# First projection of layer 1's tokens as pieces beside layer 0's last 64 scan steps, patch permutation kept in DRAM

## The chip, the core and the metric

The kernel runs on one core of a Trainium2 chip. Its engines are TensorE (PE; weight loads are listed apart as PEld), VectorE (DVE), ScalarE (ACT), GpSimd (POOL) and SyncE (SP), which issues nearly all DMAs here. Each engine works through its own instructions in order and waits on semaphores for the others. The metric is the time of one execution on the device in microseconds, as the median of the runs.

## The reference

Input x is 4 images of 128 channels and 64 x 64 pixels, all in float32. Two layers follow each other, cut here to what bears on the change.

```
# layer 0, on a group-normalised x
order = argsort of the patches' scores                   # 256 patches of 4 x 4 pixels
x1n   = layer norm of (x in that order + pe)             # (4, 4096, 128)
xm, z = split(x1n @ in_proj_w.T)                         # 256 channels each
xc    = silu(causal conv of 4 taps over xm)
dt, B, C from xc
h_t   = exp(dt_t * A) * h_{t-1} + dt_t * B_t * xc_t      # 256 channels x 16 states
y     = (sum over states of h * C + D * xc) * silu(z)
x     = x + (y @ out_proj_w.T, patches put back in place)
# layer 1, on the tokens t of x
xs, z = split(layer_norm(t) @ W_in)                      # 256 channels each
delta = xs @ W_delta ; Bv = xs @ W_B ; Cv = xs @ W_C
state_t = exp(delta_t A) * state_{t-1} + delta_t Bv_t xs_t    # 256 channels x 256 states
t = t + ((sum over channels' states with Cv) * silu(z)) @ W_out
t = t + sum over 16 filters of causal convolutions of layer_norm(t), with matrices
```

## The kernel before

The program has three stages, one after the other.

**`layer0_front`** (L24) treats the four images in turn: statistics, convolutions, scores, and from these the permutation of the 256 patches as a matrix of zeros and ones. Its transpose goes into `perm_t` (L278), a tile of all four images that stays in SBUF in the pool `ordered` until layer 0 is done. The normalised tokens in their order go to DRAM as `xnt` (L293), one write of 2 MB for each image. The order of this stage's instructions is set by a scheduler.

**`layer0_scan`** (L336) has its order written out by hand. It loads its weights (L362 to L377: `win`, `taps`, `an`, `ow` and others; L356 is the load in the helper), then runs 512 steps: 32 units of 512 tokens (4 images by 8), each in 2 halves by 8 pairs of states. A step j issues the broadcast loads of B and C for step j + 5 (`fetch`, L526), the input products for step j + 3 on GpSimd (`spread`, L540), the factors for step j + 1 on ScalarE (`lift`, L554, four instructions), and the scan of step j on VectorE (`scan`: the scan L562, the product with C L566, a small copy L567). TensorE adds the products up in PSUM (`add_up`, L578, L584), and after eight steps VectorE multiplies with the gate (`gated`, L594). The two PSUM tiles of factors alternate, so that `lift` of a step waits for the scan two steps back.

Beside each step, `beside` (L618) advances pieces of other work. Such work is a generator that says what its next piece needs: "free" (nothing), "mm" (the one PSUM tile `mm`, for a group of matmuls) or "post" (the evacuation of that tile, one step later). `fronts` are projections of the coming units (`project`, L392), which begin 9 steps ahead; `rear` is the output of finished units (`output`, L462) and the return of a finished image to its place (`put_back`, L479, with `perm_t`). One holder has the `mm` tile at a time, fronts before rear. After the last step, what is left of this runs alone (L661), and the last image's rows `om` go to DRAM as `omd` (L664, two writes of 1 MB); its return to place is made by layer 1.

**`layer1`** (L772) has an order by hand too. Its own pools lie where those of layer 0's scan lay, so that a tile's first writer waits for those who last used that place. Its weights (`layer1_weights`, L758) are loaded much earlier, into the pool `const`. Before its steps it runs the projection of the first 512 tokens without anything beside it (L1290 to L1292): `project` (L862) loads the tokens from `x2` (L867), transposes them (L871), normalises (L828), transposes back (L881), and makes gate, u, c and delta by matmuls (L889, L899, L906, L915, L921), each with its evacuation; gate and delta go to DRAM (L894, L927). Then come 8192 steps, one for each of 32 parts and 256 channels d. The rows of delta are fetched as broadcasts over 128 partitions, two to a load, eight steps ahead (L1196). GpSimd multiplies them with u (L1212), ScalarE makes the factors (L1232), VectorE scans (L1235), TensorE contracts with c (L1252). The output of the last part, layer 0's return to place, and the projection of the next part run as pieces beside these steps (L1300), and so do the spectral convolutions (L1169, L1111).

SP issues the DMAs of all this in the order of the program. A load whose place or source is not ready holds up every DMA behind it.

Of the kernel before, what the change touches and what calls it, by code (L numbers as in the profile page):

```python
# [15 lines left out]
NB = 4  # L16
L = 4096
# [6 lines left out]
def layer0_front(ctx: ExitStack, tc, ident, half, w, x, xnt, perm_t, pqd, mud):  # L24
# [161 lines left out]
    def ordered(b, xg, x1, mvx, r1, m1):  # L186
# [87 lines left out]
        for h in range(2):  # L274
            tp = ps1.tile([128, 2, 128], F32, tag="one", name="tp1")
            for k in range(2):
                nc.tensor.transpose(tp[:, k, :], perm[:, k, bass.ts(h, 128)], ident)
            nc.vector.tensor_copy(perm_t[:, b, h, :], tp.rearrange("p k j -> p (k j)"))  # L278
# [57 lines left out]
def layer0_scan(ctx: ExitStack, tc, ident, w, x, xnt, perm_t, x2, omd):  # L336
# [25 lines left out]
    win = load("win", [128, 512], w["in_proj_w"])  # L362
    taps = load("taps", [128, 4, 256], w["conv1d_w"].partition_broadcast(128))
# [23 lines left out]
    def middle():  # L387
        return ps_.tile([128, 512], F32, tag="mm", name="mm")

# [72 lines left out]
    def output(b, unit, yg, om):  # L462

        yr = yg.rearrange("p k (r o) -> p k o r", o=16)
# [14 lines left out]
    def put_back(b, om):  # L479

        for h in range(2):
# [107 lines left out]
    def gated(j):  # L589
# [5 lines left out]
        if i == PJ // SUB - 1:  # L595
            b, unit = units[n]
            if unit == 0:
                oms[b] = big.tile([128, 2, 16, 128], F32, tag="om", name="om")
            behind.append(output(b, unit, ygs.pop(n), oms[b]))
            if unit == L // PJ - 1:  # L600
                if b < NB - 1:
                    behind.append(put_back(b, oms[b]))
# [12 lines left out]
    fronts, rear, holder = [], None, None  # L615
    ahead = [1]

    def beside(j):  # L618
# [5 lines left out]
        if ahead[0] < len(units) and j >= per * (ahead[0] - 1) - 9:  # L624
            ready[ahead[0]] = tiles()
            fronts.append(Work(project(*units[ahead[0]], ready[ahead[0]])))
            ahead[0] += 1
        while fronts and fronts[0].kind is None:
# [3 lines left out]
        for work in (*fronts, rear):  # L632
            if work and work.kind == "free":
                work.next()
        for work in (*fronts, rear):
# [25 lines left out]
    while holder or rear and rear.kind or behind:  # L661
# [109 lines left out]
@with_exitstack  # L771
def layer1(ctx: ExitStack, tc, ident, half, weights, phi, pqd, mud, x, omd, permd, x2, x3, out):  # L772

# [4 lines left out]
    ctx.enter_context(tc.manual_schedule())  # L789
    wp = ctx.enter_context(tc.tile_pool(name="s_w", bufs=1))  # L790
    big = ctx.enter_context(tc.tile_pool(name="s_big", bufs=2))
    sm = ctx.enter_context(tc.tile_pool(name="s_sm", bufs=2))
    wk = ctx.enter_context(tc.tile_pool(name="s_wk", bufs=2))
    sp = ctx.enter_context(tc.tile_pool(name="s_sp", bufs=3))
    dr = ctx.enter_context(tc.tile_pool(name="s_dr", bufs=2, space=DRAM))
    pa = ctx.enter_context(tc.tile_pool(name="s_pa", bufs=1, space=PSUM))
    pm = ctx.enter_context(tc.tile_pool(name="s_pm", bufs=1, space=PSUM))
    pc = ctx.enter_context(tc.tile_pool(name="s_pc", bufs=2, space=PSUM))
    pf = ctx.enter_context(tc.tile_pool(name="s_pf", bufs=1, space=PSUM))

    win, wbd, wc, wo, at = weights
    eps = wp.tile([128, 1], F32, name="eps")
    nc.vector.memset(eps, 1e-5)
    flip = wp.tile([128, 128], F32, name="flip")
    nc.vector.memset(flip, 0.0)
    nc.gpsimd.affine_select(
        out=flip, in_=flip, compare_op=ALU.not_equal, fill=1.0, base=-127, pattern=[[1, 128]],
        channel_multiplier=1,
    )
    halos = [wp.tile([128, 2], F32, name=f"halo{i}") for i in range(2)]  # L810
    lasts = [wp.tile([128, 2, 256], F32, name=f"last{i}") for i in range(2)]
    factors = [pa.tile([128, 2, TS], F32, name=f"da{i}") for i in range(2)]
    for da in factors:
# [649 lines left out]
```

## Time and profile before

| | us |
|---|---|
| median of 3 runs | 21432.37 (21429.57 to 21440.76) |
| the profiled execution's own time | 21431.38 |
| its span, from the first instruction to the last | 21429.6 |
| VectorE busy | 20566.6 (96%) |
| GpSimd busy | 20134.2 (94%) |
| TensorE busy | 17672.7 (82%) |
| ScalarE busy | 16044.5 (75%) |
| first matmul of layer 0's scan stage (L405) | at 555.9 |
| layer 0's last scan (L562) | at 2723.5 |
| layer 1's first scan (L1235) | at 2801.4 |

Rows of the profile that are shown below read as follows. In the chain of waits: start, length, and what the end of the program hung on at that time, an instruction, a transfer, or "issue", where nothing that the profile shows was waited for. In a timeline: start, length, engine, source line, operation, output and inputs with their sizes. In a window: its stretch and length, then busy time and instructions of PE, PEld, DVE, ACT and POOL, the granted clock of TensorE as a share of full speed, the busy share of the DMA engines, and GB/s. In the list of transfers: output and source, number, size, and the median time from issue to landing. In a group: busy time, mean of one in ns, and the idle time of the engine just before them with what ended it. The source lines are those of the kernel before.

### The profile page before, as it was taken

How to read it: one execution, taken by the hardware profiler on the slowest of the kernel's cores; microseconds unless marked ns; L12 is line 12 of the kernel's file. 1: busy time of each engine (PE TensorE's matmuls, PEld its weight loads, DVE VectorE, ACT ScalarE, POOL GpSimd, SP SyncE). 2: the span in 40 equal slices, each digit the busy share in tenths (PEclk: the TensorE clock that was granted, in tenths of full speed). 3: DMA queues.
4: the chain of work that ended last, by engine and by line, in shares of the span. 5: the costliest groups of instructions: out<-in, count | busy, mean ns of one | idle time of the engine just before them, and what ended most of it. 6: DMA issues, size and time to landing. Idle time of an engine off the chain costs nothing.

```text
span 21429.6 us, 294489 instructions
## 1 busy us (share of the span) xinstructions
PE 17672.7 (82%) x99308; PEld 7756.7 (36%) x99308; DVE 20566.6 (96%) x11871; ACT 16044.5 (75%) x29620; POOL 20134.2 (94%) x5685
## 2 busy tenths in 40 slices
PE   7788854565858888886868999599999999999997
PEld 4344421222323333342323344243434434334434
DVE  7788889999999999999999999999999999999996
ACT  3777767777777777777777777787887787788875
POOL 2677789999999999999999999999999999999996
PEclk8999966776979999998979999799999999999999
DMA  1455544555756777766657777577777777777776
GB/s 69 126 139 141 140 151 153 175 179 165 218 171 221 221 224 220 221 212 191 209 181 220 230 237 236 171 236 232 237 232 229 232 234 232 233 233 230 231 231 186
DMA packets 2498780, 4302.24 MB, mean 201 GB/s; under 512 B 803272, under 2 KB 1321712, under 8 KB 2494192
## 3 DMA queue, kind: packets, MB, share of 16 engines
q1 hardware_dynamic: 2497264, 4283.40, 65.4%
q8 instruction: 784, 12.85, 0.2%
q14 instruction: 732, 6.00, 0.1%
HBM read 3658.98 MB, written 623.38 MB: 200 GB/s over the span
## 4 chain that ended last, share of the span: by engine, by line
DVE 57%; PE 14%; POOL 9%; ACT 9%; issue 8%; DMA 3%; SPq 0%; DVEq 0%; POOLq 0%; ACTq 0%
DVE s L1235 50%; POOL v L1212 8%; PE conv L1169 6%; ACT da L1232 5%; DVE states L562 3%; PE yp L1252 3%; DVE p L566 2%; PE fin L1111 1%; ACT f L554 1%; PE y L578 1%; DMA strip<-in_phi 1%; DMA dlb<-delta 1%; PE mm L471 1%; PE conv L104 0%; DVE v L1224 0%
## 5 line engine op out<-in xcount | busy, mean ns | idle before, releaser
L1212 POOL TENSOR_TENSOR v<-u,dlb 128x2044 f32<-128x2044 f32 (+1 forms) x4096 | 18244.4, 4517 | 91.7 <-DMA dlb<-delta 66.0
L1235 DVE TENSOR_TENSOR_SCAN s<-da,v 128x1024 f32<-128x1024 f32 x8192 | 18006.6, 2264 | 188.3 <-ACT da L1232 130.3
L1232 ACT ACTIVATE da<-dlb,at 128x511 f32<-128x511 f32 x16384 | 11302.9, 690 | 1990.3 <-DVE s L1235 1488.8
L1169 PE MATMUL conv<-strip,tok 128*128 128x512 f32 (+3 forms) x20480 | 8653.3, 550 | 59.0 <-DMA strip<-in_phi 58.5
L1252 PE MATMUL yp<-s,c 128*32 128x256 f32 x65536 | 4957.0, 432 | 2616.2 <-DVE s L1235 1136.7
L1169 PEld LDWEIGHTS conv<-strip,tok 128*128 128x128 f32 x20480 | 3667.2, 192 | 4156.2 <-issue 3715.8
L1252 PEld LDWEIGHTS yp<-s,c 128*32 128x32 f32 x65536 | 1964.4, 120 | 6395.3 <-issue 2085.0
L1216 ACT COPY v<-vf 128x4 f32<-128x4 f32 x4096 | 814.2, 199 | 2112.6 <-DVE s L1235 2093.6
L1111 PE MATMUL fin<-conved,pq 128*128 128x512 f32 (+1 forms) x3968 | 1793.6, 545 | 11.1 <-ACT sum L1132 5.9
L540 POOL TENSOR_TENSOR v<-dx,bcb 128x1024 f32<-128x1024 f32 x512 | 1207.2, 2358 | 436.9 <-DVE states L562 430.5
L562 DVE TENSOR_TENSOR_SCAN states<-f,v 128x1024 f32<-128x1024 f32 x512 | 1175.8, 2297 | 172.6 <-ACT f L554 123.7
L554 ACT ACTIVATE f<-dt,an 128x255 f32<-128x255 f32 x2048 | 973.5, 476 | 418.0 <-DVE states L562 367.2
L1258 ACT COPY ye<-yp 128x512 f32<-128x512 f32 x2048 | 1186.1, 579 | 23.3 <-PE yp L1252 22.6
L1181 ACT COPY conved<-conv 128x512 f32<-128x512 f32 (+1 forms) x1728 | 986.9, 571 | 236.6 <-PE conv L1169 234.0
L578 PE MATMUL y<-p,ident 128*128 128x512 f32 x2048 | 1006.7, 620 | 148.2 <-DVE p L566 143.2
L1111 PEld LDWEIGHTS fin<-conved,pq 128*128 128x128 f32 x3968 | 664.2, 192 | 384.6 <-issue 284.2
L566 DVE TENSOR_TENSOR p<-states,bcb 128x1024 f32<-128x1024 f32 x512 | 626.9, 1224 | 41.1 <-DVE states L562 3.1
L578 PEld LDWEIGHTS y<-p,ident 128*128 128x128 f32 x2048 | 369.4, 195 | 680.9 <-issue 356.3
L471 PE MATMUL mm<-ow,yg 128*32 128x128 f32 x2048 | 283.1, 298 | 106.9 <-ACT om L475 105.4
L471 PEld LDWEIGHTS mm<-ow,yg 128*32 128x32 f32 x2048 | 236.6, 139 | 213.6 <-ACT om L475 128.5
L405 PE MATMUL mm<-xin,taps 128*128 128x512 f32 x512 | 236.6, 605 | 28.3 <-DVE f L384 14.4
L447 POOL TENSOR_TENSOR e<-e,e 128x1024 f32<-128x1024 f32 x32 | 75.1, 2346 | 191.0 <-ACT e L445 191.0
(242 smaller groups left out, 5948.1 us busy)
## 6 DMA issues: line engine op xcount, KB each, us to landing
dlb<-delta SPq DMA_DIRECT2D x4096, 512.0 KB, 4.2
strip<-in_phi SPq DMA_DIRECT2D x1536, 448.0 KB, 4.8
yd<-ye SPq DMA_DIRECT2D x2048, 256.0 KB, 4.1
strip<-in_phi SPq DMA_DIRECT2D x1088, 256.0 KB, 4.4
bcb<-bcd SPq DMA_DIRECT2D x1024, 256.0 KB, 4.1
pq<-pqd SPq DMA_DIRECT2D x1472, 64.0 KB, 3.8
yt<-yd SPq DMA_DIRECT2D x4096, 4.0 KB, 3.4
pq<-pqd SPq DMA_DIRECT2D x256, 128.0 KB, 3.9
```

The lines of the kernel that those rows point to most:

```text
L540: nc.gpsimd.tensor_tensor(v, ready[n][2][:, :, bass.ts(i, SUB)].unsqueeze(1).broadcast_to((128, 2, 2, SUB)), bc[:, 0].unsqueeze(2).broadca ...
L554: nc.scalar.activation(factors[j % 2][:, a, k, 1:], ready[n][1][:, k, SUB * i + 1 : SUB * i + SUB], AF.Exp, scale=an[:, k, 2 * g + a : 2 * ...
L562: nc.vector.tensor_tensor_scan(states.rearrange(flat), factors[j % 2].rearrange(flat), v.rearrange(flat), 0.0, ALU.mult, ALU.add)
L566: nc.vector.tensor_tensor(p, states, bc[:, 1].unsqueeze(2).broadcast_to((128, 2, 2, SUB)), ALU.mult)
L578: nc.tensor.matmul(t.rearrange("p k t -> p (k t)"), ident, p[:, a].rearrange("p k t -> p (k t)"), start=g == 0 and a == 0, stop=False, ski ...
L1111: nc.tensor.matmul(fin[:, bass.ds(c0, w)], pq[:, n, :], u[:, bass.ds(c0, w)], start=begin and n == 0, stop=end and not partly, skip_group_ ...
L1169: nc.tensor.matmul(ps[:, skip:], tok[:, 1 - r if side else r, j, :], strip[:, bass.ds(c0 - lo, TS - skip)], start=which == 0 and j == js[0 ...
L1212: nc.gpsimd.tensor_tensor(v[:, 0:n, :, 1:], ready[0][:, :, 1:].unsqueeze(1).broadcast_to((128, n, 2, TS - 1)), dl[:, 0:n, 1:].unsqueeze(2) ...
L1232: nc.scalar.activation(da[:, h, 1:], dl[:, d % VD, 1:], AF.Exp, scale=at[:, h, d : d + 1])
L1235: nc.vector.tensor_tensor_scan(s[:, d % GD].rearrange("p h t -> p (h t)"), da.rearrange("p h t -> p (h t)"), v[:, d % VD].rearrange("p h t ...
L1252: nc.tensor.matmul(yp[i // 2][bass.ts(q, 32), i % 2], c[:, h, t], s[:, :, h, t], start=h == 0, stop=h == 1)
L1258: nc.scalar.copy(ye, yp[j].rearrange("p i d t -> p i t d"))
```

## The change

Layer 1's `project` and what it needs (`small`, `wide`, `normalise`, `tiles`) move out of `layer1` into a function `projection`, which is called before layer 0's scan and has pools of its own that outlive both layers. One set of the tiles u, c, vf is made there, a second one in layer 1's pool at the second part. Which PSUM tile `middle` gives is taken from a list: layer 0's `mm` first, layer 1's own later. The generator of the first projection is handed to `layer0_scan`, which starts it at step 448 as `extra`, after fronts and rear in the order of choice; `layer1` no longer runs it.

`perm_t` no longer stays in SBUF from the front. Each half of each image's transposed permutation is written to DRAM as it is made, and layer 0's scan loads all of it (1 MB) with its weights. Layer 1's weights move from the pool `const` to a pool opened after the front. The tile `om` has one buffer in place of two and is allocated in `output`.

```diff
@@ layer0_front
-            nc.vector.tensor_copy(perm_t[:, b, h, :], tp.rearrange("p k j -> p (k j)"))
+            pt = sm.tile([128, 256], F32, tag="pt", name="pt")
+            nc.vector.tensor_copy(pt, tp.rearrange("p k j -> p (k j)"))
+            nc.sync.dma_start(permd[:, b, h, :], pt)
@@ layer0_scan
     win = load("win", [128, 512], w["in_proj_w"])
+    perm_t = load("perm_t", [128, NB, 2, 256], permd)
     taps = load("taps", [128, 4, 256], w["conv1d_w"].partition_broadcast(128))
...
+    psum.append(middle)
...
-    def output(b, unit, yg, om):
+    def output(b, unit, yg):
+        if unit == 0:
+            oms[b] = big.tile([128, 2, 16, 128], F32, tag="om", name="om", bufs=1)
+        om = oms[b]
...
+        if j == steps - 64:
+            extra.append(Work(following))
...
-        for work in (*fronts, rear):
+        for work in (*fronts, rear, *extra):
             if work and work.kind == "free":
                 work.next()
-        for work in (*fronts, rear):
+        for work in (*fronts, rear, *extra):
             if work and work.kind == "mm" and holder is None:
                 work.next()
                 holder = work
...
-    while holder or rear and rear.kind or behind:
+    while holder or extra[0].kind or rear and rear.kind or behind:
         beside(steps)
@@ projection, new, around the old project
+def projection(ctx, tc, ident, half, weights, x2, psum, second):
+    first = ctx.enter_context(tc.tile_pool(name="p_1", bufs=1))
+    sm = ctx.enter_context(tc.tile_pool(name="p_sm", bufs=2))
+    dr = ctx.enter_context(tc.tile_pool(name="p_dr", bufs=2, space=DRAM))
...
     def middle():
-        return pm.tile([128, TS], F32, tag="mm", name="mm")
+        return psum[0]()
...
+    def set_of(pool):
+        return [pool.tile(shape, F32, name=name) for name, shape in (
+            ("u", [128, 2, TS]), ("c", [128, 2, TS]), ("vf", [128, 2, 256]),
+        )]
+    af = first.tile([128, 2, 256], F32, name="af")
+    sets = [set_of(first)]
+    def tiles(n):
+        if n and len(sets) < 2:
+            sets.append(set_of(second[0]))
+        u, c, vf = sets[n % 2]
...
@@ layer1
-    ready = {0: tiles()}
-    for _ in project(*parts[0], ready[0]):
-        pass
+    ready = {0: first}
@@ conv_attn_hybrid
-    with tc.tile_pool(name="ordered", bufs=1) as pool:
...
-        layer0_front(tc, ident, half, w, x, xnt, perm_t, pqd, mud)
-        weights = layer1_weights(nc, const, *(w[k] for k in ("W_in", "W_delta", "W_B", "W_C", "W_out", "A")))
...
-        nc.sync.dma_start(permd, perm_t[:, NB - 1])
-        layer0_scan(tc, ident, w, x, xnt, perm_t, x2, omd)
-    layer1(tc, ident, half, weights, w["phi"], pqd, mud, x, omd, permd, x2, x3, out)
+    layer0_front(tc, ident, half, w, x, xnt, permd, pqd, mud)
+    pool = ctx.enter_context(tc.tile_pool(name="weights", bufs=1))
+    weights = layer1_weights(nc, pool, *(w[k] for k in ("W_in", "W_delta", "W_B", "W_C", "W_out", "A")))
+    psum, second = [], []
+    work = projection(ctx, tc, ident, half, weights, x2, psum, second)
+    first = work[-2](0)
+    layer0_scan(tc, ident, w, x, xnt, permd, x2, omd, psum, work[-1](0, 0, first))
+    layer1(tc, ident, weights, work, psum, second, w["phi"], pqd, mud, x, omd, permd, first, x2, x3, out)
```

## The prediction

> **What bounds the kernel now.** I read the page's chain first, to see which stage owns the time:
>
> ```profile
> DVE s L1235 50%; POOL v L1212 8%; PE conv L1169 6%; ACT da L1232 5%; DVE states L562 3%; PE yp L1252 3%; DVE p L566 2%; PE fin L1111 1%; ACT f L554 1%; PE y L578 1%; DMA strip<-in_phi 1%; DMA dlb<-delta 1%; PE mm L471 1%; PE conv L104 0%; DVE v L1224 0%
> L1235 DVE TENSOR_TENSOR_SCAN s<-da,v 128x1024 f32<-128x1024 f32 x8192 | 18006.6, 2264 | 188.3 <-ACT da L1232 130.3
> ```
>
> Layer 1's 8192 scans (L1235) fill VectorE from 2801 us to the end: 18006.6 us busy, 188.3 us idle ahead of them. The change adds nothing to that loop. So I read the two seams: the end of layer 0's scan, and the start of that scan (where the diff adds loads). The first, as the chain of waits, gives start and length:
>
> ```profile
> 2725.90 1.24 DVE p L566
> ...
> 2740.76 0.58 ACT om L475
> 2741.36 3.85 DMA omd<-om
> ...
> 2791.56 0.32 SPq L927
> ...
> 2791.97 4.72 DMA dlb<-delta
> ...
> 2796.85 4.51 POOL v L1212
> 2801.38 2.29 DVE s L1235
> ```
>
> Layer 0's last product ends at 2727.1 and layer 1's first scan starts at 2801.4. In between lie the last output rows (to 2741.3), the write of om, the projection of layer 1's first 512 tokens, one broadcast load and one product. Between steps, layer 0's last 17 show a period of 3.81 us, with this busy time by engine (PE, PE loads, DVE, ACT, POOL):
>
> ```profile
> 2662.00:2727.00 65.00, 42.57 (x140) 19.73 (x140) 61.83 (x52) 31.21 (x66) 34.87 (x31) 1.00 0.40 114
> ```
>
> VectorE has 95%, the others about half: there is room for a projection, but not on VectorE.
>
> **Part 1, what goes: the projection at the seam.** In the changed program all pieces stand before step 497 of 512: u at steps 488 and 489, the last af at 495. Their tiles now lie outside both layers' own pools, so nothing of the projection is left at the seam. What stays is a wait: SP's first dlb load has to see both om writes landed, because dlb lies where om lay, as xq's load did before. om's second write is issued at 2741.36 and SP goes on at 2745.39 (4.03 us). Then the load 2791.97 to 2796.72 (4.75), 0.13 to start, and the product 4.51, to the scan at 0.02: 13.44 in all. First scan at 2754.80 instead of 2801.38: **-46.6 us**. Behind that waiting load on SP stand only the other dlb loads, which are wanted later. The memset and select of flip now precede the first product on VectorE and GpSimd, but end long before dlb lands. Bounds: -44.3 if the om write takes the 6.3 us of its slower half, -47.6 if the load lands in 3.7 us, the median around this seam.
>
> **Part 2, what moves: the same instructions beside the scan.** VectorE, which has no room, gets four bn_stats (0.87), four aggregates (0.36), two u (2 x 0.69) and four af (2 x 0.49): 3.6 us, counted in full. GpSimd gets 1.2 us against about 1.1 us idle in every step, with v three steps ahead: hidden. TensorE gets under 29 us in 43 steps while about a third of it is idle. SP gets five DMAs between bcb loads that run five steps ahead: hidden. ScalarE gets 13.5 us: ten copies of 0.58, two statistics 0.5, the four normalisations 1.65, silu 1.06, two table loads 2.57, vf 1.24, exp 0.63.
>
> ScalarE is where a page speaks against the change. A lift (2.0 us) may begin when the scan two steps back ends, and is needed 5.3 us later. The row of layer 0's own silu:
>
> ```profile
> 2594.86 1.28 ACT L418 ACT_TABLE_LOAD   x1
> 2596.15 1.91 ACT L418 ACTIVATE xz<-xz 128x2048 f32<-128x2048 f32 x1
> 2598.08 1.28 ACT L554 ACT_TABLE_LOAD   x1
> 2599.37 2.01 ACT L554 ACTIVATE f<-dt,an 128x255 f32<-128x255 f32 x4
> ```
>
> That is 4.5 us, and the step took 3.86 us against 3.81: no stall. The Trainium skill, "ScalarE: Activation LUTs", section "What ACT_TABLE_LOAD costs", gives about 1.28 us plus a drain of 1.38, 2.66 for every switch, and so advises to do all of one set before switching; this change puts a silu into a stream of exps. By the page its silu would cost 1.06 + 5.3 = 6.4 us and overrun ScalarE's slack of 3.3 us plus the 1.8 us that each step frees, by about 1.3 us. By the row no such drain appears (load 1.28, next instruction 0.01 later): 1.06 + 2.57 = 3.6 us, hidden. I take the row. A nearer measure of everything together: steps 480 to 496, with a unit's projection, took 64.3 us, and the next 16, without, about 61.7; that projection has some 13 us of ScalarE and 9.4 of GpSimd, and costs 2.6, nearly all of it at its Ln pair. The new pieces have no Ln; I take 0.9 us for them. Sum **+4.5 us**; bounds 3.6 (VectorE alone) and 17 (all of ScalarE's 13.5 exposed as well).
>
> **Part 3, what is added at the other seam: the start of layer 0's scan.** DMA queue of the stretch 500 to 620, median us to landing, and SP's wait:
>
> ```profile
> xnt<-xn SPq DMA_DIRECT2D x1, 2049.5 KB, 8.6
> xin<-xnt SPq DMA_DIRECT2D x2, 257.5 KB, 2.8
> taps<-in_conv1d_w SPq DMA_DIRECT2D x1, 512.0 KB, 9.0
> cb<-in_conv1d_b SPq DMA_DIRECT2D x1, 1.0 KB, 8.3
> SPq L397 <- DMA taps<-in_conv1d_w: 0.4, 1, 0.4
> ```
>
> One KB took 8.3 us because it stood behind 2 MB: the loads drain about in order. Here all engines wait: xnt is issued at 542.73 and landed by 551.3, taps at 552.65, xin is issued at 552.66 and TensorE begins at 555.91. The change puts three things in this path. Layer 1's five weight loads (1.125 MB) leave the first 25 us, where nothing waited for them, and stand behind xnt. perm_t (1 MB, new) stands ahead of taps. And layer 0's win now lies over the old xn tile, so its load, and every one behind it on SP, waits for xnt's landing; before, they were issued under it. So win, perm_t and taps (1.75 MB) start at 551.3, behind what is left of the weights. At 430 GB/s (the rate of the loads at the start) they drain by 556.6, at 270 (this stretch) by 560; with 1.7 us from last byte to landing, taps is there at 558.3 to 561.7. xin waits for taps (0.4 to issue, 2.8 to land): TensorE begins at 561.6 to 565.3. **+5.7 to +9.4, taken +7.5 us.** The ten issues (nine took 6.5 us before, and perm_t's) end at about 558 and are not the later limit. It cannot be much under +4: the wait for xnt is in the program.
>
> The eight small permd writes of the front (128 KB each) stand ahead of writes that wait longer for ScalarE: nothing. One om buffer instead of two: output and put_back were already one queue, nothing. perm_t resident or loaded is the same operand to put_back.
>
> **Sum**: -46.6 + 4.5 + 7.5 = -34.6 us. Against the profiled execution: span 21429.6 to 21395.0, its time 21431.4 (1.8 around the span) to 21396.8. The median of the three runs is 21432.4, 1.0 above; I forecast that minus 34.6: **21398 us**, or -0.16%. About 0.2% (43 us) is what a measurement of this kernel can tell from no change: the forecast lies inside it.
>
> **Rivals.**
> - *The pieces cost what their ScalarE time is.* If their copies fall where ScalarE is already late (the Ln pair delayed the scan by about 2 us in each unit), up to 17 us go in the 64 steps: -46.6 + 17 + 7.5 = -22, **21410**. For: VectorE waited for f 6.6 us in the last 65 steps. Against: those waits lie at six scans alone. 0.15.
> - *Both losses are hidden*: the start overlaps (SP's issues were stretched by a full queue, and taps comes in time), the pieces cost 3.6: -43, **21389**. Against: the ordered wait on xnt. 0.10.
> - *The long loop changes its pace, and the kernel is slower.* u, c, vf and the small tiles sit at other addresses, and the loop starts without the 70 us pause (granted clock 1.00 before it, 0.62 in 2800 to 2900). It decides from 34.6 us / 8192 = 4.2 ns a scan (0.19% of 2264); at 7 ns it gives +57 - 35 = +22, **21455**. Against: VectorE is 98.6 to 100% busy there at a clock of 0.6, so the clock has no say, and the loop's order of instructions is the same in both programs. 0.05.
> - *The moved part is not moved*: pieces left over at the end would run at the seam. The program's order excludes it; within the first rival.
>
> **Numbers.** Forecast 0.70, with its own 21390 to 21404. Range 21386 to 21413, which takes in the bounds of the parts and the first two rivals. Faster than 21389.5 (0.2%): 0.10, the second rival. Slower than 21475: 0.02, a part of the third, whose rest stays within. Within 0.2%: 0.88.
>
> **What would show it.** Right: from layer 0's last output copy to the first L1235 scan some 13.5 us (60.0 before); the first L405 matmul 6 to 9 us later than 555.9, SP's load of win waiting for xnt; the 64 steps 4 to 6 us longer, with bn_stats, u and af between the scans; the scans' mean still 2264 ns. Wrong: a first dlb load that waits for more than om; f late at more than the six scans; another mean at L1235.

## The result, and the profile after

| | before | changed |
|---|---|---|
| median, us | 21434.19 (21429.57 to 21441.05, 9 runs) | 21379.17 (21368.94 to 21383.9, 9 runs) |
| ratio | | 0.9972, 95% interval 0.9964 to 0.9981 |
| profiled execution, its time (span) | 21431.38 (21429.6) | 21379.17 (21377.5) |
| front's last copy (ScalarE) to layer 0's first taps matmul | 13.2 | 19.1 |
| layer 0's last 64 scans, first start to last start | 251.8 | 253.0 |
| layer 0's last scan to layer 1's first scan | 77.9 | 30.6 |
| layer 1's first scan to its last scan | 18448.2 | 18437.8 |
| last scan's end to the end | 177.8 | 171.4 |

The changed kernel is 55.0 us faster, a little over a quarter of a per cent. The forecast was 21398 us with a range that began at 21386 and a chance of 0.88 for "within 0.2%": the time fell under the range, and the gain is larger than 0.2%. The rows from the fourth on are differences of starts and ends in the two traces.

On the page of the changed kernel, the chain by line and the two largest groups (busy time, mean of one in ns, then idle time ahead and its cause):

```profile
DVE s L1261 50%; POOL v L1238 8%; PE conv L1195 7%; ACT da L1258 5%; PE yp L1278 3%; PE fin L1137 1%; DMA dlb<-delta 1%; DMA strip<-in_phi 1%; DMA yd<-ye 0%; DVE v L1250 0%; ACT ye L1284 0%; PE mm L1052 0%; ACT t L820 0%; PE mm L884 0%; DVE st L805 0%
...
L1238 POOL TENSOR_TENSOR v<-u,dlb 128x2044 f32<-128x2044 f32 (+1 forms) x4096 | 18223.6, 4518 | 66.2 <-DMA dlb<-delta 42.9
L1261 DVE TENSOR_TENSOR_SCAN s<-da,v 128x1024 f32<-128x1024 f32 x8192 | 18008.3, 2286 | 187.8 <-ACT da L1258 132.0
```

The picture is the old one, and the second line holds what the forecast did not weigh. It stood on the page before as well:

```profile
L1212 POOL TENSOR_TENSOR v<-u,dlb 128x2044 f32<-128x2044 f32 (+1 forms) x4096 | 18244.4, 4517 | 91.7 <-DMA dlb<-delta 66.0
```

GpSimd's 4096 products fill 18223.6 us with 66.2 us idle ahead of them, against 187.8 us ahead of the scans; before, it was 91.7 against 188.3. The chain does not tell who leads: it gives half of the time to the scans and 8% to the products. Both engines look full; here the one with less idle time sets the pace, as the experiments show.

The chain of waits at the end of layer 0 in the changed kernel (start, length, what):

```profile
2737.80 1.24 DVE p L575
...
2752.65 0.59 ACT om L483
2753.24 0.02 issue
2753.25 3.86 DMA omd<-om
...
2757.32 3.96 DMA dlb<-delta
...
2761.53 4.50 POOL v L1238
...
2766.06 0.04 DVE s L1261
```

The projection is gone from it. From the last copy of om to the first scan it takes 12.8 us: the store, one broadcast load, one product. The forecast had 13.4.

ScalarE beside the last 64 steps, in the timeline of the changed kernel (start, length, engine, line, operation, how many), at the moved silu:

```profile
2582.91 1.28 ACT L871 ACT_TABLE_LOAD   x1
2584.20 1.06 ACT L871 ACTIVATE t<-t 128x1024 f32<-128x1024 f32 x1
2585.28 1.28 ACT L563 ACT_TABLE_LOAD   x1
2586.57 3.93 ACT L563 ACTIVATE f<-dt,an 128x255 f32<-128x255 f32 x8
```

From the first table load to the first factor of the scan 3.66 us pass: 1.06 of silu and two loads of 1.28. No further pause stands at either switch. The row was the right choice against the 2.66 us a switch of the Trainium skill ("ScalarE: Activation LUTs", "What ACT_TABLE_LOAD costs").

At the start of layer 0's scan (stretch 500 to 620), the transfers of the changed kernel with KB and median us to landing:

```profile
xnt<-xn SPq DMA_DIRECT2D x1, 2049.5 KB, 8.3
perm_t<-permd SPq DMA_DIRECT2D x1, 1024.0 KB, 5.7
xin<-xnt SPq DMA_DIRECT2D x2, 257.5 KB, 2.9
taps<-in_conv1d_w SPq DMA_DIRECT2D x1, 512.0 KB, 6.6
```

and the waits of SP's queue there (line, what for, us in total, how often, longest):

```profile
SPq L358 <- DMA xnt<-xn: 2.9, 1, 2.9
SPq L358 <- DMA perm_t<-permd: 1.6, 1, 1.6
SPq L402 <- DMA taps<-in_conv1d_w: 1.0, 1, 1.0
```

By SP's own timeline it is win that stands 2.9 us for the landing of xnt, ow 1.6 us for that of perm_t, and xin 1.0 us for that of taps. The wait for xnt was forecast, and taps in front of xin. What the forecast did not see is a pattern: ow is the eighth load behind perm_t, and xin the eighth behind taps. Before, `an`, the eighth behind xnt, stood 2.2 us for xnt, and xin, again the eighth behind taps, 0.4 us. In after_start (below) ow is the eighth behind taps and waits for it (0.6 us), while xin, right behind taps, is issued at 554.36 without a wait. So win waits for its place, as forecast, and the other waits go by the place in SP's row.

Up to layer 1's first scan the changed kernel is 35.3 us ahead (2801.38 to 2766.06). 3.6 us of the other sign lie in the front, to which the change adds the writes of permd. They are spread and no cost of it: over the profiles of this study the front's last copy ends at 542.7 to 547.7 without the change and at 542.8 to 549.3 with it, with a median of 546.1 in both. The other 17 us lie inside layer 1, where the order of instructions is the same on every engine: 10.4 in the loop, 6.4 in the tail (after the last scan). These were the open question.

### The profile page after: what moved, and what is told of

Read it like the earlier page. It is cut to its first block, busy times and chain, and to the rows that moved or that the text cites. A ratio compares the mean times of both kernels' runs of the same rounds, so it can differ in the third digit from the quotient of the medians.

```text
span 21377.5 us, 294496 instructions
## 1 busy us (share of the span) xinstructions
PE 17653.8 (83%) x99308; PEld 7751.4 (36%) x99308; DVE 20559.4 (96%) x11871; ACT 16041.0 (75%) x29620; POOL 20113.6 (94%) x5685
## 4 chain that ended last, share of the span: by engine, by line
DVE 51%; PE 12%; POOL 8%; issue 7%; ACT 6%; DMA 2%; SPq 0%; DVEq 0%; POOLq 0%; ACTq 0%
DVE s L1261 50%; POOL v L1238 8%; PE conv L1195 7%; ACT da L1258 5%; PE yp L1278 3%; PE fin L1137 1%; DMA dlb<-delta 1%; DMA strip<-in_phi 1%; DMA yd<-ye 0%; DVE v L1250 0%; ACT ye L1284 0%; PE mm L1052 0%; ACT t L820 0%; PE mm L884 0%; DVE st L805 0%
## 5 line engine op out<-in xcount | busy, mean ns | idle before, releaser
L1238 POOL TENSOR_TENSOR v<-u,dlb 128x2044 f32<-128x2044 f32 (+1 forms) x4096 | 18223.6, 4518 | 66.2 <-DMA dlb<-delta 42.9
L1261 DVE TENSOR_TENSOR_SCAN s<-da,v 128x1024 f32<-128x1024 f32 x8192 | 18008.3, 2286 | 187.8 <-ACT da L1258 132.0
L1137 PE MATMUL fin<-conved,pq 128*128 128x512 f32 (+1 forms) x3968 | 1786.6, 543 | 10.4 <-ACT sum L1158 5.3
L571 DVE TENSOR_TENSOR_SCAN states<-f,v 128x1024 f32<-128x1024 f32 x512 | 1175.9, 2297 | 173.8 <-ACT f L563 125.6
```

The costliest lines, as they stand in the source:

```text
L571: nc.vector.tensor_tensor_scan(states.rearrange(flat), factors[j % 2].rearrange(flat), v.rearrange(flat), 0.0, ALU.mult, ALU.add)
L1137: nc.tensor.matmul(fin[:, bass.ds(c0, w)], pq[:, n, :], u[:, bass.ds(c0, w)], start=begin and n == 0, stop=end and not partly, skip_group_ ...
L1238: nc.gpsimd.tensor_tensor(v[:, 0:n, :, 1:], ready[0][:, :, 1:].unsqueeze(1).broadcast_to((128, n, 2, TS - 1)), dl[:, 0:n, 1:].unsqueeze(2) ...
L1261: nc.vector.tensor_tensor_scan(s[:, d % GD].rearrange("p h t -> p (h t)"), da.rearrange("p h t -> p (h t)"), v[:, d % VD].rearrange("p h t ...
```

## The experiments

Layer 1's loop starts some 4096 products on GpSimd. "v period" below is the median distance between the starts of two of them, in ns, taken from each trace over the parts of the loop that read the first tile of u (even) and the second (odd). "Seam" is the distance from layer 0's last scan to layer 1's first.

**Is it the placement?** The change moves layer 1's tiles in SBUF. First the kernel before with nothing but that.

```diff
-    wp = ctx.enter_context(tc.tile_pool(name="s_w", bufs=1))
-    big = ctx.enter_context(tc.tile_pool(name="s_big", bufs=2))
+    p1 = ctx.enter_context(tc.tile_pool(name="p_1", bufs=1))
     sm = ctx.enter_context(tc.tile_pool(name="s_sm", bufs=2))
+    wp = ctx.enter_context(tc.tile_pool(name="s_w", bufs=1))
+    big = ctx.enter_context(tc.tile_pool(name="s_big", bufs=1))
...
+    af = p1.tile([128, 2, 256], F32, name="af")
+    sets = [set_of(p1)]
+    def tiles(n):
+        if n and len(sets) < 2:
+            sets.append(set_of(big))
+        u, c, vf = sets[n % 2]
```

> The kernel before, order untouched, with layer 1's tiles (u, c, vf, af, t2, t4, flip, last, yt) at the very SBUF addresses that they have in the changed kernel. Theory P (the addresses set the pace of layer 1's loop): the median period of GpSimd's v products falls from 4.487 to 4.481 us, the mean duration of the layer-1 scan rises from 2264 to about 2286 ns, the stretch from the first layer-1 scan to the end falls by 10 to 17 us, and the time is 10 to 17 us under before, near 21419. Theory Q (the loop is quicker because it starts without the pause at the seam) and theory R (the pace differs from one execution to the next by chance): no difference from before, within 5 us.

Then the changed kernel with its tiles in place and its projection at the seam again.

```diff
-    layer0_scan(tc, ident, w, x, xnt, permd, x2, omd, psum, work[-1](0, 0, first))
+    layer0_scan(tc, ident, w, x, xnt, permd, x2, omd, psum, iter(()))
...
     ready = {0: first}
+    for _ in project(*parts[0], first):
+        pass
```

> The changed kernel with its tiles, weights and DRAM tensors where they are, but with the first projection of layer 1 in front of its scan again, one piece behind the other, and nothing beside the last 64 steps of layer 0. All theories: first layer-1 scan 45 to 49 us later than in the changed kernel, at about 2813. Theory P: pace of the loop as in the changed kernel (v period 4.481, scan 2286 ns), so about 21425, near 9 us under before. Theory Q: pace of the kernel before (v period 4.487), so about 21442, some 8 us over before. Theory R: in between, and its own profile's pace follows neither.

And each kernel once more:

> The changed kernel once more, to see what another execution gives. Theories P and Q: v period 4.481 us and scan 2286 ns again, layer 1 from its first scan to the end within 4 us of the first profile's 18611, about 55 us under before. Theory R: the pace moves by several ns a product, and the lead over before falls anywhere from 35 to 60 us.

> The kernel before, unchanged, beside itself. Theories P and Q: v period 4.487 us, scan 2264 ns, layer 1 from its first scan to the end within 4 us of 18628, time within 3 us of before. Theory R: the pace moves by several ns a product, and layer 1 by 10 us or more.

| on one chip | median, us | seam | v period, even / odd | loop | tail |
|---|---|---|---|---|---|
| before (36 runs) | 21442.13 | | | | |
| before_again | 21438.19 | 76.4 | 4487 / 4487 | 18461.2 | 171.7 |
| before_layout | 21427.77 | 78.2 | 4483 / 4480 | 18437.7 | 181.1 |
| after_serial | 21424.38 | 70.4 | 4483 / 4480 | 18441.0 | 174.3 |
| after_again | 21381.35 | 30.8 | 4484 / 4480 | 18433.5 | 175.7 |

Theory P holds: with the changed kernel's addresses the period is the same to a nanosecond whether the projection stands at the seam or not, and with the old ones it is 4487. Q falls with after_serial, which has the pause and the quick loop. R falls for the period, which repeats to 1 ns, and holds for the rest: the tail goes from 171.7 to 181.1 with no pattern, so the 6.4 us of the first comparison can't be put down to the change; and the loop of the kernel before took 18448.2 in one execution and 18461.2 in another, 13 us apart, so one pair of traces does not show a gain of 10 in the loop either. That is also why before_again lay outside what P and Q expected of it (3.9 us under before where at most 3 was expected, and 18635 us from the first layer-1 scan to the end where 18624 to 18632 was). The intervals of the time reach 1 for before_layout (0.9985 to 1.0001) and after_serial (0.9984 to 1.0000), so that here too the period carries the proof. One more expectation of P failed: the mean scan of 2286 ns did not come back (2265 or 2266 in all four). It was that one execution's and has nothing to do with the pace.

after_serial also splits the seam. Its chain, from the last output matmul on:

```profile
2749.71 1.98 PE mm L479 x16
2751.68 0.08 issue
2751.76 0.17 DVE flip L955
...
2752.07 0.68 DVE st L805 x3
2752.75 0.29 DVE mv L807 x4
```

In the kernel before, the same stretch behind om's last store:

```profile
2745.20 3.07 issue
2748.27 1.10 PE mm L871 x4
...
2750.13 0.87 DVE st L833 x4
```

There the load of the tokens waited for om's stores, and the statistics of the projection (st) start 8.8 us after the last copy of om; in after_serial they start before that copy has ended. The seam is 70.4 us in place of 76.4 to 78.2, where 45 to 49 us more than the changed kernel's 30.6 had been expected: some 6 to 8 us of the gain come from the projection's tiles lying apart, the other 40 from the projection being moved.

**Which tile?** GpSimd's product reads u and dlb and writes v; of these only u had moved.

Both kernels make layer 1's tiles by name, in an order that puts u where it is wanted. layout_u has u at 28448 and 58240:

```diff
+    eps, last0, u0 = tile(wp, "eps", 1), tile(wp, "last0", 2, 256), tile(wp, "u0", 2, TS)
...
+    cs = [tile(wp, f"c{i}", 2, TS) for i in range(2)]
+    vfs = [tile(wp, f"vf{i}", 2, 256) for i in range(2)]
+    us, af = [u0, tile(wq, "u1", 2, TS)], tile(wq, "af", 2, 256)
```

layout_not_u has u at 31072 and 35168, and the others elsewhere:

```diff
+    eps, af, vf0, flip = tile(wp, "eps", 1), tile(wp, "af", 2, 256), tile(wp, "vf0", 2, 256), tile(wp, "flip", 128)
...
+    us = [tile(wp, f"u{i}", 2, TS) for i in range(2)]
+    lasts = [tile(wp, f"last{i}", 2, 256) for i in range(2)]
+    cs = [tile(wq, f"c{i}", 2, TS) for i in range(2)]
+    vfs = [vf0, tile(wq, "vf1", 2, 256)]
```

> The kernel before with its order untouched; of layer 1's tiles the two of u (the operand that GpSimd's product, its relief on VectorE and nothing else in the loop read) lie where the changed kernel has them, the others elsewhere near their old places. Theory U (u's addresses set the pace): v period 4.481 to 4.482 us, layer 1 from its first scan to the end 7 to 17 us shorter than the kernel before's 18628 to 18635, time 10 to 15 us under before. Theory N (another tile than u sets it): v period 4.487, time within 4 us of before.

> The kernel before with its order untouched; u stays at its old addresses, and every other one of layer 1's tiles in that region (c, vf, af, last, yt, t2, t4) is moved. Theory U: v period 4.487 us, time within 4 us of before. Theory N: the period leaves 4.487, to 4.481 or anywhere else.

layout_u: 4484 / 4481 ns, 21430.09 us against 21442.38 (ratio 0.9993, 0.9985 to 1.0002). layout_not_u: 4488 / 4488, 21442.03 (ratio 1.0000). So it is u. The interval of the time alone would not settle it; the period does. That layout_u's own profiled loop (18446.1) is hardly shorter than before's is the spread seen above.

**What of its address?** Even and odd parts of one execution differ (4483 and 4480), and 28448 and 58240 differ modulo 128. That was the next theory.

In the kernel before (before_align), eps and halos behind u:

```diff
+    we = ctx.enter_context(tc.tile_pool(name="s_we", bufs=1))
...
-    eps = wp.tile([128, 1], F32, name="eps")
+    eps = we.tile([128, 1], F32, name="eps")
-    halos = [wp.tile([128, 2], F32, name=f"halo{i}") for i in range(2)]
+    halos = [we.tile([128, 2], F32, name=f"halo{i}") for i in range(2)]
```

In the changed kernel (after_align), halos in front of the first u:

```diff
-    halos = [wp.tile([128, 2], F32, name=f"halo{i}") for i in range(2)]
...
+    halos = [first.tile([128, 2], F32, name=f"halo{i}") for i in range(2)]
     sets = [set_of(first)]
```

> The kernel before with its order untouched; only eps and the two halo tiles (96 bytes) go behind u, c, af, vf and yt, so that those lie 96 bytes lower: the two tiles of u at 30976 and 35072 in place of 31072 and 35168, which is 0 in place of 96 modulo 128. Theory A (what counts of u's address is its place within 128 bytes; so far 96 went with a median v period of 4487, 32 with 4483 to 4484, 0 with 4480): 4480 ns in even and odd parts, time 12 to 20 us under before. Theory D (the distance between u's two tiles, or between them and the tiles it is multiplied with, counts): 4487, time within 4 us of before.

> The changed kernel with the halo tiles (64 bytes) in front of its first u, which so lies at 28512 in place of 28448 (96 in place of 32 modulo 128); the second u stays at 58240 (0). Theory A: the median v period of even parts, which read the first u, rises from 4483 to 4487, that of odd parts stays at 4480; the time rises 4 to 8 us over the changed kernel's 21379 to 21381. Theory D: even parts stay at 4483.

before_align: 4488 / 4488, 21442.50 against 21440.25. after_align: 4487 / 4480, 21385.94. The second came out as theory A said, the first against it, so A fell. A third kernel has both seams altered (as in after_both, below) and its u at 28416 and 58176:

```diff
+    late = ctx.enter_context(tc.tile_pool(name="p_2", bufs=1))
...
-    eps = first.tile([128, 1], F32, name="eps")
+    eps = late.tile([128, 1], F32, name="eps")
...
-    halos = [wp.tile([128, 2], F32, name=f"halo{i}") for i in range(2)]
+    halos = [we.tile([128, 2], F32, name=f"halo{i}") for i in range(2)]
```

> The kernel with both seams altered, and eps and the halo tiles behind u: the first u at 28416 (0 modulo 128), the second at 58176 (64 modulo 128). Theory A: even parts 4480; odd parts between 4480 and 4487, whichever 64 goes with (4480 if a line of 64 bytes is what counts, 4485 if a product slows with every 32 bytes); time within 4 us of the kernel with both seams altered alone.

both_align: 4488 / 4486, 21378.59 us; the same kernel with u at 28448 and 58240 has 4483 / 4480 and 21364.31 on the same chip. The place of u in the same program is worth 14 us.

By now five places modulo 256 were seen. Either that place counted, or u's distance to the tiles it is multiplied with; dlb, v and s lie on 128 modulo 256 in all kernels so far.

Both kernels have both seams altered. both_256 has 96 bytes more in front of the first u:

```diff
+    sv = ctx.enter_context(tc.tile_pool(name="p_v", bufs=2))
     first = ctx.enter_context(tc.tile_pool(name="p_1", bufs=1))
...
-        ve = sm.tile([128, NT], F32, tag="ve", name="ve")
+        ve = sv.tile([128, NT], F32, tag="ve", name="ve")
...
+    halo = first.tile([128, 2], F32, name="halo0")
```

both_shift has 128 bytes in front of dlb, v and s:

```diff
+    pad = ctx.enter_context(tc.tile_pool(name="s_pad", bufs=1))
+    pad.tile([128, 32], F32, name="pad")
     wk = ctx.enter_context(tc.tile_pool(name="s_wk", bufs=2))
```

> The kernel with both seams altered, with 96 bytes of small tiles in front of its first u, which lies at 28544 in place of 28448; the second stays at 58240. Modulo 256 that is 128 for both, where the broadcast and product tiles lie too (68480, 84864). Theory E (the place within 256 bytes counts; so far 0 went with 4488, 32 with 4483, 64 with 4486, 96 with 4487 to 4488, 128 with 4480): even parts 4480 like the odd ones, time 0 to 6 us under the kernel with both seams altered alone. Theory F (no rule on low bits; 58240 is quick for where it lies): even parts 4483 or over.

> The kernel with both seams altered, u where it was (28448 and 58240), and 128 bytes in front of the broadcast, product and scan tiles, which so lie at 0 in place of 128 modulo 256 (68608, 84992). If u's place against those tiles counts: odd parts, now half of 256 apart, 4488 in place of 4480, even parts something other than 4483, time up to 14 us over the kernel with both seams altered alone. If u's own place counts: 4483 and 4480 as before.

both_256: 4481 / 4481, 21366.0. both_shift: 4476 / 4489, 21368.46. Moving the other tiles and not u turned the quick set into the slow one and the other into the quickest yet: the distance counts. (The pad moves what lies behind dlb, v and s as well; but of all these the product touches only dlb and v.) Then a distance of 32 for both sets at once, and the two distances not yet seen, each as both_256 with a pad in front of dlb, v and s (56 words; 48 for a distance of 64, 40 for 96). "Theory R" is the distance from here on:

```diff
+    pad = ctx.enter_context(tc.tile_pool(name="s_pad", bufs=1))
+    pad.tile([128, 56], F32, name="pad")
     wk = ctx.enter_context(tc.tile_pool(name="s_wk", bufs=2))
```

> The kernel with both seams altered, u at 28544 and 58240, broadcast, product and scan tiles 224 bytes higher (68704, 85088): u lies 32 bytes past them modulo 256. Theory R (the distance of u from the tiles it is multiplied with, modulo 256, sets the period; so far 0 went with 4480, 32 with 4476, 160 with 4483, 128 with 4488, 192 with 4486, 224 with 4487): 4476 in even and odd parts, time 5 to 12 us under the kernel with both seams altered alone, near 21355. If the 4476 was the first address's own: even and odd parts differ.

> As the run with a distance of 32, with 64 bytes between the places modulo 256. Theory R: even and odd parts alike; the value itself is not known, between 4476 and 4488 if it follows its neighbours.

> As the run with a distance of 32, with 96 bytes between the places modulo 256. Theory R: even and odd parts alike, between 4476 and 4488.

Against 21429.25 us for the kernel before on that chip: both_d32 21341.63 (ratio 0.9958, 0.9945 to 0.9972), both_d64 21571.25 (1.0068, 1.0054 to 1.0082), both_d96 21357.49 (0.9968, 0.9956 to 0.9980). All places together, as the distance from dlb to u modulo 256:

| distance | 0 | 32 | 64 | 96 | 128 | 160 | 192 | 224 |
|---|---|---|---|---|---|---|---|---|
| v period, ns | 4480 to 4481 | 4476 | 4540 to 4541 | 4480 to 4481 | 4488 to 4489 | 4483 to 4484 | 4486 | 4487 to 4488 |
| where | changed, odd | both_d32 | both_d64 | both_d96 | before_align | changed, even | both_align, odd | before |

The values for 64 and 96 come from one trace each, that for 192 from half of one; the others were seen in two kernels or more. The expected "between 4476 and 4488" for 64 was wrong by 52 ns. GpSimd's row in the timeline at the same place of the loop (start, length of a row of products with nothing between them, how many), for the kernel before, the changed one, both_d32 and both_d64:

```profile
9327.10 76.33 POOL L1212 TENSOR_TENSOR v<-u,dlb 128x2044 f32<-128x2044 f32 x17
```

```profile
9283.27 76.26 POOL L1238 TENSOR_TENSOR v<-u,dlb 128x2044 f32<-128x2044 f32 x17
```

```profile
9251.29 76.20 POOL L1251 TENSOR_TENSOR v<-u,dlb 128x2044 f32<-128x2044 f32 x17
```

```profile
9336.86 77.34 POOL L1251 TENSOR_TENSOR v<-u,dlb 128x2044 f32<-128x2044 f32 x17
```

Seventeen products take 76.33, 76.26, 76.20 and 77.34 us. The rows are unbroken: it is the product that is longer, not a wait between two. The page's mean of one (4517 before, 4518 in the changed kernel) doesn't show the 6 ns between these two; the distance of starts does.

A rival is that the product itself is the same and the scan beside it holds it up at some places. The traces speak against it as the whole cause. In each of three traces, 36 to 39 products stand beside scans that fill less than 52% of the time to the next product; the median of that time is there 4469 ns in the kernel before, 4457 in before_d32 (below) and 4525 in both_d64. A product beside fewer scans is 15 to 20 ns quicker in each, but the differences between the places remain. Products with no scan at all beside them are too few to settle it.

Who sets whose pace is seen in the group of scans over the stretch 3000 to 21000 (count, busy, mean, idle ahead by cause) of both_d32 and both_d64:

```profile
L1274 DVE TENSOR_TENSOR_SCAN s<-da,v 128x1024 f32<-128x1024 f32 x8003 | 17572.9, 2269 | 173.7 <-ACT da L1271 139.0 <-POOL v L1251 26.2
```

```profile
L1274 DVE TENSOR_TENSOR_SCAN s<-da,v 128x1024 f32<-128x1024 f32 x7901 | 17458.9, 2271 | 285.6 <-ACT da L1271 126.7 <-POOL v L1251 58.7
```

A slower product leaves the scan as long as it was (2269 and 2271 ns) and puts idle time ahead of it (173.7 and 285.6 us): VectorE waits, GpSimd does not. The windows of the same stretch (PE, PE loads, VectorE, ScalarE, GpSimd busy; clock, DMA share, GB/s) of before and both_d64 agree:

```profile
3000.00:21000.00 18000.00, 15054.99 (x89834) 6414.05 (x89835) 17815.40 (x8880) 13871.15 (x25649) 17943.60 (x4232) 0.92 0.69 214
```

```profile
3000.00:21000.00 18000.00, 14941.63 (x88803) 6351.64 (x88804) 17707.78 (x8789) 13714.53 (x25357) 17956.86 (x4185) 0.91 0.68 212
```

GpSimd is 99.7% busy in the one and 99.8% in the other, VectorE 99.0 and 98.4.

Last, the distance alone, with no part of the change:

```diff
+    pad = ctx.enter_context(tc.tile_pool(name="s_pad", bufs=1))
+    pad.tile([128, 48], F32, name="pad")
     wk = ctx.enter_context(tc.tile_pool(name="s_wk", bufs=2))
```

> The kernel before with 192 unused bytes in front of its broadcast, product and scan tiles and nothing else altered: u (31072, 35168) lies 32 past them modulo 256 in place of 224. Theory R: median v period 4476 in place of 4487 in even and odd parts, both seams as before (78 us at the end of layer 0), time 20 to 28 us under before, as the step from a distance of 0 and 160 to one of 32 brought about 22. If the gain needs the changed kernel's other places: within 5 us of before.

4476 / 4476 ns, seam 78.2 us as before, 21405.37 us against 21441.08: 35.7 us less (ratio 0.9985, 0.9976 to 0.9994), somewhat over the expected 20 to 28. One unused tile brings nearly two thirds of what the whole change brings (55.0 us).

**The two seams.** What is left at each was tried by taking it away.

after_start, in the changed kernel's layer0_scan (the loads from cb to ow move behind the first tokens' load, `next(start)`; layer 1's weight loads become a function):

```diff
-    perm_t = load("perm_t", [128, NB, 2, 256], permd)
+    perm_t = cp.tile([128, NB, 2, 256], F32, name="perm_t")
...
-    for _ in project(*units[0], ready[0]):
+    start = project(*units[0], ready[0])
+    next(start)
+    cb = halves("cb", w["conv1d_b"])
...
+    for _ in start:
         pass
+    nc.sync.dma_start(perm_t, permd)
+    weight_loads()
```

after_end, in the changed kernel (ow, yg and om in the new pool behind b_wk; flip is made in projection):

```diff
+    ob = ctx.enter_context(tc.tile_pool(name="b_out", bufs=2))
...
-            oms[b] = big.tile([128, 2, 16, 128], F32, tag="om", name="om", bufs=1)
+            oms[b] = ob.tile([128, 2, 16, 128], F32, tag="om", name="om", bufs=1)
...
-        nc.sync.dma_start(omd[h], oms[NB - 1][:, h])
+        nc.scalar.dma_start(omd[h], oms[NB - 1][:, h])
...
+    flip = first.tile([128, 128], F32, name="flip")
```

after_both is the two together.

> The changed kernel with the loads at the head of layer 0's scan in another order: its input projection weights, taps and the first tokens first, the other constants behind them, and the patch permutation and layer 1's weights only behind the first projection. If the loads in front of the first tokens are what the start of layer 0's scan costs (step 3 of the forecast, 6.0 us by the traces): first taps matmul about 6 us earlier than the changed kernel's 565.5, at 559 to 560, and the time 5 to 7 us under the changed kernel. If the landing of the tokens' transposed write sets it (it ends 3.3 us later there): 0 to 3 us.

> The changed kernel with the last unit's gated products, the output weights and the output tile in a pool that layer 1's broadcast buffers don't take the place of, the two stores of that tile issued by ScalarE, and the flip matrix made beside layer 1's projection: the first broadcast load of layer 1 no longer waits for the stores (12.8 us from the last copy to the first scan in the changed kernel: store 3.86, load 3.96, product 4.50). If that chain is what is left at the seam: first broadcast load near 2743 in place of 2757.3, seam from the last layer-0 scan to the first layer-1 scan 19 to 21 us in place of 30.7, and the time 9 to 14 us under the changed kernel. If other work is as late (the copies of the output on ScalarE in front of the first decay factors), the gain stays under 4 us.

> The changed kernel with both seams altered as before: loads at the head of layer 0's scan in the other order (5.9 us earlier from the front's last copy to the first taps matmul when alone), and the first broadcast load of layer 1 free of the stores (seam 19.8 in place of 30.7 us when alone). If they add up: front's last copy to first taps matmul 13 us, seam 19.8 us, time 15 to 18 us under the changed kernel, near 21364. If one gives back what the other brings: over 21370.

after_start: from the front's last copy to the first taps matmul 12.9 us in place of 19.1, 21377.31 us (before, same chip: 21442.38). after_end: seam 19.8 in place of 30.6, 21374.30 us. after_both: 12.6 and 19.8 us, 21364.31 against 21440.25 (ratio 0.9964, 0.9952 to 0.9977). They add up, and the time came out at the 21364 that was written down. The chain of after_end at the seam:

```profile
2746.25 0.59 ACT om L485
...
2746.86 0.33 ACTq L674
...
2747.43 0.60 ACT da L1260
...
2748.05 0.70 ACT da L1260
...
2748.83 3.80 DVE s L1263 x2
```

Load and product have left the chain. What is late now is ScalarE: the last copy of om, the stores' issue and the first two decay factors, 2 us from copy to scan. after_end is 68.1 us under before where after_again is 60.8, 7 us for a seam 11 us shorter, where 9 to 14 were expected; after_start gains 4 for 6, where 5 to 7 were expected. These two have six runs each, which spread over 15 to 19 us. after_both, 75.9 under before, is 15 us ahead of after_again for some 17 taken from the two seams.

The kernel that beats both is both_d32: both seams altered and the distance at 32. It is 87.6 us under the kernel before, where the changed kernel is 55.0.

## Why the prediction was wrong

- **Part 1, the projection at the seam, -46.6.** Right: -47.2 (77.87 to 30.65). The om wait, the load and the product are the chain that was named; the load took 3.96 in place of 4.75.
- **Part 2, the pieces beside the scan, +4.5.** Right in kind, too large: 251.8 to 253.0 us, +1.2, and against after_serial, which has the new places but no pieces (252.6), +0.4. Over all traces of this study the kernels with the pieces have 252.8 to 254.4 us and those without 251.8 to 252.6, so the pieces cost 0.2 to 2.6 us, less than the forecast's lower bound. VectorE's "3.6 us, counted in full" is what was mis-sized. The 95% came from the 17 steps at the end; over the whole stretch of the kernel before (2482.5 to 2723.5), VectorE is busy for 220.7 us of 241.0. The forecast had the idle time of the wrong steps: the pieces lie in the earlier ones. There (steps 448 to 496) VectorE is busy 2.8 us longer in the changed kernel than in after_serial (178.5 and 175.7) and idle 2.0 us less. ScalarE's silu cost what the row said.
- **Part 3, the loads at the start, +7.5.** Right, within its bounds: +5.9 (13.2 to 19.1), and after_start takes it away, though it moves perm_t, the weights and xin's place in SP's row at once and so does not part them. The upper end of the forecast should read +9.1 by its own terms (taps at 561.7, and 3.3 us from there to TensorE as before), not +9.4.
- **Their sum** is -40.1 where -34.6 was forecast. Alone it would have given some 21392, inside the range. Parts 2 and 3 both erred to the slow side.
- **The step that failed** is the term put at nothing: "The change adds nothing to that loop", and with it the third rival's answer, in two places. The rival asked whether the long loop changes its pace because "u, c, vf and the small tiles sit at other addresses", and put that aside because "VectorE is 98.6 to 100% busy there at a clock of 0.6, so the clock has no say, and the loop's order of instructions is the same in both programs". The clock and the order were answered, the addresses were not. And VectorE's share was read as the bound although GpSimd's products were as full, with less idle time ahead of them (91.7 us against 188.3); so the forecast did not ask whether a product could take another time at another place. It also had one sign only: slower. The runs put in its place that the product takes 4487 ns before and 4480 to 4484 after, by the distance of u from dlb and v. On its own this brings 12 to 14 us (layout_u 12.3, before_layout 14.4, each against before on its chip). With -40.1 that makes -52 to -54, against the -55.0 measured. In the repetition the changed kernel was 60.8 us under before, 6 to 9 us more than this sum; the interval of the first ratio alone spans 41 to 77 us, so the closeness alone proves little.

Open: whether the distance that counts is that to dlb or that to v, since the two always moved together; what makes it so; and why of a change in the period times 4096 only half to nine tenths reach the time (before_d32: 11 ns are 45 us, 35.7 came). A part of the last can be read in the traces: a quicker GpSimd pauses more often. Distances of over 4750 ns between two products, with nothing else of GpSimd's between, number 28 in both_d64, 36 and 41 in the two traces of the kernel before, 53 in before_d32 and 54 in both_d32; what they have above the period comes to 44, 47 and 57, 60 and 67 us.

## What to carry to other kernels

Where two engines both look full, look for the one with less idle time ahead of its instructions: here it set the pace, and the distance between its starts, not the mean of one, showed a change of a tenth of a per cent. A change that moves tiles can alter the time of untouched loops: when forecasting, list which operands of the pacing instruction move, and when measuring, repeat the kernel with the old order at the new places before crediting the order. For a GpSimd product of two SBUF tiles try the operands' places against each other modulo 256; here one unused tile was worth nearly two thirds of a restructuring.

## What the runs showed of the hardware

- The time of GpSimd's product of 2 x 2 x 511 elements a partition follows the distance of u from its other operands modulo 256 bytes: 4476 to 4489 ns at seven of eight distances in steps of 32 bytes, and 4540 at a distance of 64, which cost 0.68% of the whole kernel against before, and some 219 us against both_256, which differs by the pad alone (each against before on its own chip). The Trainium skill, "SBUF — State Buffer", section "Operand start alignment", asks for a multiple of the element size alone and says that its runs timed nothing; all eight places meet that.
- The mean scan of one execution was 2286 ns where the other profiles have 2261 to 2271, with no effect on the pace of its loop. It was not the scan alone: all of VectorE's records in layer 1 are some 20 to 30 ns longer there than in the kernel before, whatever their length (bn_stats 297 against 271, aggregate 177 against 150, u 686 against 661), while those of layer 0 are the same (scan 2297 in both). Here such a shift of the records meant nothing for the time.
- On SP a load waited for the landing of the one eight places ahead of it in the row, in three traces at the start of layer 0's scan (2.2 and 0.4 us before, 1.6 and 1.0 in the changed kernel, 0.6 in after_start); whether the chip or the program makes it so is not shown.
- The last stretch of the kernel, after the last scan, took 171.4 to 181.1 us over twenty profiles, whatever the kernel.
